# Moving roots, layernorm applications and a residual add between GpSimd, ScalarE and VectorE in a macaron block

## The chip, the cores and the metric

The kernel runs on one core of a Trainium2 chip. A core has five engines that matter here: TensorE (PE in the profile, with its weight loads as PEld), VectorE (DVE), ScalarE (ACT), GpSimd (POOL) and SyncE (SP), which here only issues DMAs. The metric is the device time of one execution in microseconds. The kernel before takes 2504.11 us, the median of three runs (2503.69 to 2505.66).

## The reference: a feed-forward part, attention, a feed-forward part

The input x has 8 batches of 1024 rows of 512 fp32 values. The block computes

```python
x = x + 0.5 * ffn(layernorm(x))
x = x + attention(layernorm(x))
x = x + 0.5 * ffn(layernorm(x))
```

`layernorm` subtracts the mean of a row and divides by the root of its variance plus 1e-5. `ffn` quantises each row and each column of a 512 x 512 matrix to whole numbers between -127 and 127, with the largest absolute value as the scale, multiplies them, and scales the product back by the row's and the column's scale. `attention` projects to q, k and v with 16 heads of 32 values, applies a layernorm with gain and offset to each head of q and k, takes the causal softmax of the scaled products, and projects the result with a bias.

## The kernel before, in words

**Tiles.** A tile is 128 rows of x. `First` (L317) is the first feed-forward part of a tile and the layernorm ahead of attention, `Last` (L353) is attention's output projection and the second feed-forward part, and both inherit the quantised product from `Ffn` (L258). `Norm` (L231) holds a layernorm: `stats` on VectorE, `root` on GpSimd, `apply` on VectorE. `Unit` (L386) is attention for four heads of one batch; there are 32 units. A unit's work has three phases that run in three successive stages: projection of q, k and v with their norms (`project`, `take`, `squares`, `logs`, `divide`, `turn`), row maxima of the scores (the `m_` functions), and exponentials with sums (the `e_` functions).

**Order.** The order on each engine is the program's, written out by hand. Each engine works through its own list in that order. After an opening loop for ten `First` tiles (L680 to L704) comes a plan of stages k = -1 to 32 of 20 steps each (L737 to L836). Stage k runs the `e_` phase of unit k, the `m_` phase of unit k+1 and the projection of unit k+2. `at(k, s, rank, fn)` puts a function at a step; one with a step past 19 falls into the next stage. Inside a step the order is by rank, FILL, SUM, MISC, REST, BULK, ADD, and inside a rank by the order of the calls to `at`.

For the change, this is who stands where:

- FILL: scores of both phases on TensorE, then `m_max` (VectorE), the exponential (ScalarE, L589) and, on diagonal blocks, the causal select (GpSimd, L593).
- SUM: `e_sum` (the product with v, L621) in even steps, and `e_den` (L635) in steps 10 and 22, that is 2 of the next stage. `e_den` writes `p_d` and copies it out on ScalarE (L647).
- MISC: `turn` (L452) in steps 11, 13, 21 and 23; `flip` (L296), `product` (L303) and `spread` (L345) of the feed-forward tiles.
- REST: everything else of the tiles and norms. BULK: projections. ADD: `e_add` (GpSimd, L609) and, in steps 17 and 18, `m_wide`, `m_turn`, `m_shift`.

A stage has two `First` tiles for k = -1 to 25 and two `Last` tiles for k = 4 to 31. Stages 4 to 25 have both.

**Buffers.** PSUM is divided by tags. `ps_e` and `ps_m` hold scores, `ps_p` (two buffers) projections. `ps_x` (L199) is one bank with one buffer. `turn`, `e_den`, and in the stages also `flip`, `product` and `spread` of all tiles but those of the last batch take it in turn: each user's first matmul waits until the engine that reads the user before it has finished.

Of the kernel before, what the change touches and what calls it, by code (L numbers as in the profile page):

```python
# [9 lines left out]
F32 = mybir.dt.float32  # L10
# [5 lines left out]
P = 128  # L16
# [39 lines left out]
def macaron_kernel(  # L56
# [51 lines left out]
    nc.vector.memset(ones_bf, 1.0)  # L108
    eps = const.tile([P, 1], F32, name="eps")
    nc.vector.memset(eps, EPS)  # L110
    mhalf = const.tile([P, 1], F32, name="mhalf")
    nc.vector.memset(mhalf, -0.5)
# [118 lines left out]
    class Norm:  # L231
# [26 lines left out]
    class Ffn:  # L258
# [44 lines left out]
        def product(self):  # L303
# [5 lines left out]
            self.f = self.tile([P, E], F32, "f")  # L309
            nc.vector.scalar_tensor_tensor(self.f, p_f, self.hsc, rs_bc, ALU.mult, ALU.mult)  # L310

        def add(self):
            nc.gpsimd.tensor_tensor(self.f, self.f, self.src, ALU.add)  # L313

# [71 lines left out]
    class Unit:  # L386
# [44 lines left out]


        def logs(self, j):
            lv = small.tile([P, 16], F32, tag="hlv", name=f"hlv_{self.u}_{j}")
            nc.scalar.activation(lv, self.ss, AF.Ln, scale=1.0 / HD, bias=eps)
            self.r0 = small.tile([P, 16], F32, tag="hr0", name=f"hr0_{self.u}_{j}")
            nc.scalar.activation(self.r0, lv, AF.Exp, scale=-0.5)

        def divide(self, j):
            tag = f"{self.u}_{j}"  # L440
            ss, r0, c = self.ss, self.r0, self.cs[j]
            nc.vector.tensor_scalar(ss, ss, 1.0 / HD, EPS, ALU.mult, ALU.add)
            h = small.tile([P, 16], F32, tag="hh", name=f"hh_{tag}")
            nc.vector.scalar_tensor_tensor(h, r0, -0.5, r0, ALU.mult, ALU.mult)
            nc.vector.tensor_tensor(h, h, ss, ALU.mult)
            r = small.tile([P, 16], F32, tag="hr", name=f"hr_{tag}")
            nc.vector.scalar_tensor_tensor(r, h, 1.5, r0, ALU.add, ALU.mult)
            c = c.rearrange("p t s d -> p (t s) d")
            nc.vector.tensor_tensor(c, c, r.unsqueeze(2).to_broadcast([P, 16, HD]), ALU.mult)

# [245 lines left out]
    for j in range(NT // 2):  # L696
        for i, fn in ((15, "squares"), (15, "logs"), (16, "divide"), (17, "turn")):
            extra[2 * j + i].append((getattr(units[0], fn), j))
# [45 lines left out]
    def last(f, k, s0):  # L744
        at(k, s0, BULK, f.project, 0)
        at(k, s0 + 1, BULK, f.project, 1)
        for s, rank, fn in (
            (-1, REST, f.load),
            (2, REST, f.begin),
            (3, REST, f.root),  # L750
            (4, REST, f.scale),
            (5, REST, f.whole),
            (6, MISC, f.flip),
            (7, MISC, f.product),
            (8, REST, f.add),
            (9, REST, f.store),
# [3 lines left out]
    for k in range(-1, NU + 1):  # L760
# [44 lines left out]
        if 0 < b < B and (b, j) != (1, 0):  # L805
            for n in range(2):
                f = First(b, 2 * j + n, ps_x, bufs)
                for s, rank, fn in (
                    (2, REST, f.load),
                    (4, REST, f.begin),  # L810
                    (5, REST, f.root),
                    (6, REST, f.scale),
                    (7, REST, f.whole),
                    (8, MISC, f.flip),
                    (9, MISC, f.product),
                    (10, REST, f.add),
                    (11, REST, f.store),
# [60 lines left out]
```

## Time and profile before

| | us |
|---|---|
| median of three runs | 2504.11 |
| the profiled execution | 2508.39 |
| its span | 2506.7 |
| PE busy | 2392.0 (95%) |
| DVE busy | 1778.8 (71%) |
| POOL busy | 1681.9 (67%) |
| ACT busy | 1237.1 (49%) |

Instructions that the change touches, by line and mean duration:

| Line | What | Count | Mean, ns |
|---|---|---|---|
| L251 | layernorm applied, DVE: tile's input, before attention, second part | 64 each | 640, 978, 599 |
| L310 | product scaled out of PSUM, DVE | 128 | 744 |
| L313 | residual added, POOL | 128 | 1405 and 1420 |
| L435, L437 | logarithm and exponential for the norm's root, ACT, 16 columns | 128 each | 322, 216 |
| L442, L444, L445, L447 | refinement of that root, DVE, 16 columns | 128 each | 216, 194, 259, 483 |
| L248 | a power on POOL, one column | 192 | 572 to 577 |
| L535 | row maxima spread for the transposes, ACT | 32 | 1056 |

Busy times are sums of instruction durations; they can overlap on TensorE, where matmuls are pipelined. A wait is listed with the engine and line that ended it. In the middle of the execution a stage takes 73.6 us and stages repeat to within a few hundredths of a microsecond.

### The profile page before, as it was taken

What the parts mean: (1) busy time and instruction counts of PE and PEld (TensorE: products, weight loads), DVE (VectorE), ACT (ScalarE), POOL (GpSimd) and SP (SyncE); (2) the same over time, 40 slices, a digit from 0 to 9 for tenths busy, and PEclk for the clock granted to TensorE, in tenths of its full rate; (3) what the DMA queues carried; (4) which work ended last, traced back from release to release, by engine and by line L of the source; (5) the groups of instructions that cost most, each with busy time, mean ns of one, the idle gap of its engine ahead of it and who ended that gap; (6) DMA issues with size and microseconds to landing.
All of it is one profiled execution on the core that took longest, in us unless ns stands there. A gap on an engine that the chain in (4) does not pass through costs nothing.

```text
span 2506.7 us, 40820 instructions
## 1 busy us (share of the span) xinstructions
PE 2392.0 (95%) x15448; PEld 1099.6 (44%) x15448; DVE 1778.8 (71%) x3053; ACT 1237.1 (49%) x2409; POOL 1681.9 (67%) x1790
## 2 busy tenths in 40 slices
PE   3999999999999999999999999999999999999785
PEld 1544444444444444444444444444444444444332
DVE  9566777777777777777777777777777776666664
ACT  2335555555554555555555555555555555545441
POOL 3227777776777776677777667777767776666672
PEclk9899999999999999999999999999999999999997
DMA  4000000111110111111011111111111100000011
GB/s 143 30 18 22 27 26 27 31 41 38 33 42 31 43 35 35 39 35 43 31 43 35 35 39 35 43 32 35 44 35 39 35 28 25 27 27 27 26 43 59
DMA packets 79303, 92.86 MB, mean 37 GB/s; under 512 B 30977, under 2 KB 37121, under 8 KB 79106
## 3 DMA queue, kind: packets, MB, share of 16 engines
q1 hardware_dynamic: 79106, 90.26, 11.8%
q8 instruction: 121, 1.98, 0.3%
q14 instruction: 76, 0.62, 0.1%
HBM read 55.60 MB, written 34.08 MB: 36 GB/s over the span
## 4 chain that ended last, share of the span: by engine, by line
PE 76%; DVE 12%; POOL 7%; issue 4%; SPq 1%; ACT 1%; DMA 1%; DVEq 0%; POOLq 0%; ACTq 0%
PE p_qkv L402 22%; PE p_s L496 17%; PE p_o L621 9%; PE p_w_b L370 8%; PE p_t L566 6%; POOL pt L609 4%; DVE nm L523 3%; PE p_f_b L306 2%; PE p_d L639 2%; PE p_s L480 2%; PE p_f_a L306 2%; PE p_h L456 2%; POOL f_b L313 2%; DVE oT L674 1%; PE p_m L543 1%
## 5 line engine op out<-in xcount | busy, mean ns | idle before, releaser
L609 POOL TENSOR_TENSOR pt<-pt,pt 128x768 f32<-128x768 f32 (+1 forms) x630 | 1109.7, 1764 | 127.0 <-ACT pt L589 108.5
L589 ACT ACTIVATE pt<-p_t 128x1024 f32<-128x1024 f32 (+1 forms) x640 | 599.4, 938 | 982.4 <-PE p_t L566 908.4
L523 DVE TENSOR_REDUCE nm<-p_s 128x2 f32<-128x1024 f32 (+2 forms) x640 | 632.9, 1006 | 525.8 <-PE p_t L566 409.6
L402 PE MATMUL p_qkv<-wall,yT_a 128*128 128x384 f32 x2048 | 773.7, 501 | 0.2 <-ACT v L421 0.2
L496 PE MATMUL p_s<-qk 32*128 32x512 f32 (+3 forms) x3072 | 656.6, 524 | 14.1 <-DVE nm L523 12.4
L566 PE MATMUL p_t<-qk 32*128 32x512 f32 (+3 forms) x3072 | 663.2, 526 | 2.0 <-ACT pt L589 2.0
L402 PEld LDWEIGHTS p_qkv<-wall,yT_a 128*128 128x128 f32 x2048 | 354.7, 191 | 287.3 <-issue 136.6
L593 POOL TENSOR_SCALAR_AFFINE_SELECT pt<-pt 128x256 f32<-128x256 f32 x512 | 227.6, 457 | 215.6 <-ACT pt L589 214.2
L621 PE MATMUL p_o<-pt,v 128*32 128x512 f32 (+3 forms) x3072 | 340.7, 497 | 11.8 <-POOL pt L593 11.6
L496 PEld LDWEIGHTS p_s<-qk 32*128 32x128 f32 x3072 | 227.5, 185 | 198.0 <-DVE nm L523 65.6
L566 PEld LDWEIGHTS p_t<-qk 32*128 32x128 f32 x3072 | 238.7, 183 | 52.2 <-ACT pt L589 23.5
L370 PE MATMUL p_w_b<-wo,oT 128*128 128x512 f32 x512 | 244.3, 600 | 0.0
L621 PEld LDWEIGHTS p_o<-pt,v 128*32 128x32 f32 x3072 | 75.1, 108 | 247.8 <-issue 159.0
L313 POOL TENSOR_TENSOR f_a<-f_a,xin_a 128x512 f32<-128x512 f32 x64 | 90.9, 1420 | 84.2 <-DVE f_a L310 84.2
L480 PEld LDWEIGHTS <-ident_bf 128*128 128x128 bf16 x1024 | 83.5, 98 | 135.9 <-issue 81.2
L462 ACT ACTIVATE qk<-p_h,qk_b,qk_g 128x256 f32<-128x256 f32 x256 | 130.1, 563 | 11.9 <-PE p_h L456 11.9
L370 PEld LDWEIGHTS p_w_b<-wo,oT 128*128 128x128 f32 x512 | 97.6, 192 | 78.0 <-issue 69.1
L480 PE MATMUL p_s<-causal_bf,ident_bf 128*128 128x128 bf16 x1024 | 110.2, 220 | 8.6 <-DVE nm L523 5.8
L514 DVE TENSOR_REDUCE nm<-p_s 128x4 f32<-128x1024 f32 x64 | 77.6, 1212 | 47.2 <-PE p_t L566 42.6
L417 ACT ACTIVATE sq<-p_qkv 128x256 f32<-128x256 f32 x256 | 99.1, 387 | 21.7 <-PE p_qkv L402 15.1
L420 ACT COPY c<-p_qkv 128x256 f32<-128x256 f32 x256 | 96.8, 378 | 4.3 <-PE p_h L456 4.3
L313 POOL TENSOR_TENSOR f_b<-f_b,x_b 128x512 f32<-128x512 f32 x64 | 89.9, 1405 | 8.9 <-DVE f_b L310 8.9
(108 smaller groups left out, 2474.0 us busy)
## 6 DMA issues: line engine op xcount, KB each, us to landing
xin_a<-in_x_dram SPq DMA_DIRECT2D x64, 256.0 KB, 2.8
x1d_a<-f_a SPq DMA_DIRECT2D x64, 256.0 KB, 2.2
rb<-rdr SPq DMA_DIRECT2D x256, 64.0 KB, 2.0
x1r_b<-x1d_a SPq DMA_DIRECT2D x64, 256.0 KB, 2.9
out_dram<-f_b SPq DMA_DIRECT2D x64, 256.0 KB, 2.1
dsq<-dsb SPq DMA_DIRECT2D x256, 2.0 KB, 1.7
rT<-in_rhsT_dram SPq DMA_DIRECT2D x4, 256.0 KB, 3.6
wall<-in_wqT_dram SPq DMA_DIRECT2D x4, 256.0 KB, 5.8
```

Source lines behind the costliest of these rows:

```text
L313: nc.gpsimd.tensor_tensor(self.f, self.f, self.src, ALU.add)
L370: nc.tensor.matmul(self.p_w, oT[self.b, g, hf][:, o : o + P], wo[:, g, :], start=False, stop=(g == NG - 1),)
L402: nc.tensor.matmul(self.p[:, : 3 * P], yT[self.b, t][:, kc, :], wall[:, kc, self.g].rearrange("p a f -> p (a f)"), start=(kc == 0), stop=( ...
L462: nc.scalar.activation(self.qk[:, a, 2 * j * P : (2 * j + 2) * P], p_h[:, a].rearrange("p t i -> p (t i)"), AF.Identity, scale=qk_g[:, a : ...
L480: nc.tensor.matmul(self.pm[:, hh, c0 + n - P : c0 + n], ident_bf, causal_bf, start=not self.pm_begun, stop=False, skip_group_check=True,)
L496: nc.tensor.matmul(self.pm[:, hh, c0 : c0 + n], self.rows(0, h, it * P, P), self.rows(1, h, ch * HALF, n), start=not self.pm_begun and sub ...
L523: nc.vector.tensor_reduce(self.nm[:, ch, it, hs], self.pm[:, :, c0 : c0 + n], AX.X, ALU.max, negate=True)
L566: nc.tensor.matmul(self.pes[pr][:, hh, c0 : c0 + n], self.rows(1, h, jt * P, P), self.rows(0, h, hf * HALF + o, n), start=True, stop=True, ...
L589: nc.scalar.activation(pt[:, :, :cols], self.pes[pr][:, :, :cols], AF.Exp, scale=scale)
L593: nc.gpsimd.affine_select(out=pt[:, :, c0 : c0 + P], in_=pt[:, :, c0 : c0 + P], compare_op=ALU.is_ge, fill=0.0, base=0, pattern=[[0, 2], [ ...
L609: eng.tensor_tensor(acc[:, :, o : o + n], acc[:, :, o : o + n], pt[:, :, c0 : c0 + n], ALU.add)
L621: nc.tensor.matmul(self.p_o[h * HD : (h + 1) * HD, o : o + n], self.v[:, jt, h * HD : (h + 1) * HD], self.pt[i, h // 2][:, h % 2, c0 : c0 ...
```

## The change

There are three exchanges between engines and a re-timing that goes with them.

1. `logs` and the refinement in `divide` are replaced by `roots`, which adds the epsilon and takes the power -0.5 of 16 columns on GpSimd. `divide` keeps only its last multiplication.
2. `Norm.apply` becomes one ScalarE instruction with scale rstd and a per-row offset; `root` computes this offset on GpSimd. In the feed-forward part `apply` moves out of `scale` into a step of its own, `norm`, and all that follows, up to `product`, comes one step later.
3. `add` on GpSimd goes. `product` multiplies the PSUM tile in place by the column scales and then, in a second VectorE instruction, by the row scale with the residual added. `store` keeps its step.
4. `m_wide` moves from step 17 (last rank) to step 18 (MISC).

```diff
         def root(self):
-            nc.gpsimd.tensor_tensor(self.rstd, ve, mhalf, ALU.pow)
+            nc.gpsimd.tensor_tensor(self.rstd, ve, mhalf[:, 0:1], ALU.pow)
+            self.off = small.tile([P, 1], F32, tag="off", name=f"off_{self.tag}", bufs=8)
+            nc.gpsimd.tensor_scalar(
+                self.off, self.mv[:, 0:1], self.rstd, -1.0, ALU.mult, ALU.mult
+            )
         def apply(self, dst):
-            nc.vector.tensor_scalar(
-                dst, self.src, self.mv[:, 0:1], self.rstd, ALU.subtract, ALU.mult
-            )
+            nc.scalar.activation(dst, self.src, AF.Identity, scale=self.rstd, bias=self.off)
...
+        def norm(self):
+            self.y = self.tile([P, E], F32, "y")
+            self.ln.apply(self.y)
         def scale(self):
-            self.y = self.tile([P, E], F32, "y")
-            self.ln.apply(self.y)
...
-            nc.vector.scalar_tensor_tensor(self.f, p_f, self.hsc, rs_bc, ALU.mult, ALU.mult)
-        def add(self):
-            nc.gpsimd.tensor_tensor(self.f, self.f, self.src, ALU.add)
+            nc.vector.tensor_tensor(p_f, p_f, rs_bc, ALU.mult)
+            nc.vector.scalar_tensor_tensor(self.f, p_f, self.hsc, self.src, ALU.mult, ALU.add)
...
-        def logs(self, j):
-            lv = small.tile([P, 16], F32, tag="hlv", name=f"hlv_{self.u}_{j}")
-            nc.scalar.activation(lv, self.ss, AF.Ln, scale=1.0 / HD, bias=eps)
-            self.r0 = small.tile([P, 16], F32, tag="hr0", name=f"hr0_{self.u}_{j}")
-            nc.scalar.activation(self.r0, lv, AF.Exp, scale=-0.5)
+        def roots(self, j):
+            ve = small.tile([P, 16], F32, tag="hve", name=f"hve_{self.u}_{j}")
+            nc.gpsimd.tensor_scalar(ve, self.ss, 1.0 / HD, EPS, ALU.mult, ALU.add)
+            self.r = small.tile([P, 16], F32, tag="hr", name=f"hr_{self.u}_{j}")
+            nc.gpsimd.tensor_tensor(self.r, ve, mhalf, ALU.pow)
         def divide(self, j):
-            nc.vector.tensor_scalar(ss, ss, 1.0 / HD, EPS, ALU.mult, ALU.add)
-            nc.vector.scalar_tensor_tensor(h, r0, -0.5, r0, ALU.mult, ALU.mult)
-            nc.vector.tensor_tensor(h, h, ss, ALU.mult)
-            nc.vector.scalar_tensor_tensor(r, h, 1.5, r0, ALU.add, ALU.mult)
             nc.vector.tensor_tensor(c, c, r.unsqueeze(2).to_broadcast([P, 16, HD]), ALU.mult)
...
-    parts = "load begin root scale whole flip product add store root2 norm2 spread".split()
+    parts = "load begin root norm scale whole flip product store root2 norm2 spread".split()
...
     def last(f, k, s0):
-            (4, REST, f.scale), (5, REST, f.whole),
-            (6, MISC, f.flip), (7, MISC, f.product), (8, REST, f.add),
+            (4, REST, f.norm), (5, REST, f.scale), (6, REST, f.whole),
+            (7, MISC, f.flip), (8, MISC, f.product),
             (9, REST, f.store),
...
-            at(k, 17, ADD, mu.m_wide)
+            at(k, 18, MISC, mu.m_wide)
...
-                at(k, s + 2, REST, pu.logs, j)
+                at(k, s + 2, REST, pu.roots, j)
...
     (First, in the stages)
-                    (6, REST, f.scale), (7, REST, f.whole),
-                    (8, MISC, f.flip), (9, MISC, f.product), (10, REST, f.add),
+                    (6, REST, f.norm), (7, REST, f.scale), (8, REST, f.whole),
+                    (9, MISC, f.flip), (10, MISC, f.product),
                     (11, REST, f.store), (12, REST, f.root2), (13, REST, f.norm2),
                     (16, MISC, f.spread),
```

More of the change, by code (lines that the diff above doesn't have):

```diff
@@ L108, in macaron_kernel @@
     nc.vector.memset(ones_bf, 1.0)
-    eps = const.tile([P, 1], F32, name="eps")
-    nc.vector.memset(eps, EPS)
-    mhalf = const.tile([P, 1], F32, name="mhalf")
+    mhalf = const.tile([P, 16], F32, name="mhalf")
     nc.vector.memset(mhalf, -0.5)
@@ L430, in squares @@
             )
[L433 to L449 removed]
+        def roots(self, j):
[3 more added lines that the diff above has]
+            nc.gpsimd.tensor_tensor(self.r, ve, mhalf, ALU.pow)
+        def divide(self, j):
+            c = self.cs[j].rearrange("p t s d -> p (t s) d")
+            nc.vector.tensor_tensor(
+                c, c, self.r.unsqueeze(2).to_broadcast([P, 16, HD]), ALU.mult
+            )
         def turn(self, j):
@@ L696, in macaron_kernel @@
     for j in range(NT // 2):
-        for i, fn in ((15, "squares"), (15, "logs"), (16, "divide"), (17, "turn")):
+        for i, fn in ((15, "squares"), (15, "roots"), (16, "divide"), (17, "turn")):
             extra[2 * j + i].append((getattr(units[0], fn), j))
@@ L750, in last @@
             (3, REST, f.root),
[L751 to L755, printed above, removed]
+            (4, REST, f.norm),
+            (5, REST, f.scale),
+            (6, REST, f.whole),
+            (7, MISC, f.flip),
+            (8, MISC, f.product),
             (9, REST, f.store),
@@ L811, in macaron_kernel @@
                     (5, REST, f.root),
[L812 to L816, printed above, removed]
+                    (6, REST, f.norm),
+                    (7, REST, f.scale),
+                    (8, REST, f.whole),
+                    (9, MISC, f.flip),
+                    (10, MISC, f.product),
                     (11, REST, f.store),
```

## The prediction, made before the changed kernel had run

> **What bounds the kernel now.** I read the row of busy tenths on the page first, then busy times by stretch of time, then the timelines of single engines inside one stage, because the row alone can't say whether a busy TensorE is merely waiting inside its pipeline. The columns of the second fence are the stretch, its length, and busy time (with counts) of PE, PEld, DVE, ACT and POOL.
>
> ```profile
> PE   3999999999999999999999999999999999999785
> ```
>
> ```profile
> 218.50:284.50 66.00, 64.40 (x450) 29.48 (x448) 47.48 (x76) 36.16 (x73) 47.58 (x49) 1.00 0.09 26
> 1444.50:1518.00 73.50, 72.90 (x483) 33.76 (x482) 54.19 (x94) 38.36 (x75) 53.07 (x57) 1.00 0.12 37
> 2180.00:2253.00 73.00, 73.00 (x482) 33.72 (x484) 45.90 (x74) 35.56 (x70) 49.05 (x49) 1.00 0.08 23
> ```
>
> TensorE is busy for all but 0.6 us of a 73.5 us stage; VectorE has 19 us free, GpSimd 20, ScalarE 35. In the PE timeline of one stage (start, duration, instruction) each group starts where the one before stops feeding, some 0.07 us ahead of its listed end:
>
> ```profile
> 1418.67 1.06 PE L621 MATMUL p_o<-pt,v 128*32 128x512 f32 x8
> 1419.56 1.04 PE L639 MATMUL p_d<-pt,ones 128*32 128x512 f32 x8
> 1420.53 1.56 PE L402 MATMUL p_qkv<-wall,yT_a 128*128 128x384 f32 x4
> ...
> 1431.87 0.70 PE L496 MATMUL p_s<-qk 32*128 32x512 f32 x2 [0.19 <-DVE nm L523]
> ...
> 1440.13 1.06 PE L621 MATMUL p_o<-pt,v 128*32 128x512 f32 x8
> 1441.13 0.66 PE L348 MATMUL p_y_a<-ident,y_a 128*128 128x128 f32 x4
> 1441.62 1.46 PE L402 MATMUL p_qkv<-wall,yT_a 128*128 128x384 f32 x4
> ```
>
> Measured that way, PE loses only 0.79 us in the stage from 1370 to 1444: 0.13 and 0.26 waiting for a row maximum (the second is the marked line), and 0.40 waiting for GpSimd's causal select, in step 18. POOL's timeline shows why: the residual add and a sum stand ahead of that select.
>
> ```profile
> 1369.65 1.55 POOL L313 TENSOR_TENSOR f_b<-f_b,x_b 128x512 f32<-128x512 f32 x1
> 1371.16 2.35 POOL L609 TENSOR_TENSOR pt<-pt,pt 128x1024 f32<-128x1024 f32 x1
> 1373.47 0.78 POOL L593 TENSOR_SCALAR_AFFINE_SELECT pt<-pt 128x256 f32<-128x256 f32 x2
> ```
>
> So in the middle, busy time taken from VectorE can return at most 0.79 us a stage. A new PE wait, however, adds its full length. The two ScalarE lines that decide are these:
>
> ```profile
> 1420.66 0.59 ACT L647 COPY dsb<-p_d 128x512 f32<-128x512 f32 x1 [0.74 <-PE p_d L639]
> ...
> 1441.82 0.59 ACT L350 COPY yT_a<-p_y_a 128x512 f32<-128x512 f32 x1 [0.42 <-PE p_y_a L348]
> ```
>
> They empty `ps_x`, while PE is already on p_qkv, which has another bank.
>
> **What the Trainium skill says.** PSUM — Partial Sum Buffer, section Engine vs sequencer instructions: matmuls start and complete in program order, and the other engines' queues are strict FIFO. The timelines agree: the 0.40 us wait above has everything of PE behind it. The same page, section PSUM bank collisions raise a hardware error, asks that a bank be guarded as a whole, so a second tile in the one `ps_x` bank can't begin under the first one's copy. ScalarE: Activation LUTs, section What ACT_TABLE_LOAD costs, prices an activation at 186 ns plus 0.833 ns an element and about 93 ns for each pointer operand. The trace agrees: 378 ns for a plain copy of 256 columns (L420), 563 with two pointers (L462), so 92 each. GPSIMD Engine Reference, section 3.1, makes GpSimd's cost per element grow with the operations that an element takes; it prices no power.
>
> **The change part by part, in a stage with both kinds of tile.**
>
> *Work moved.* VectorE loses 2 x 0.64 + 2 x 0.98 + 2 x 0.60 = 4.4 us (L251) and 4 x (0.22 + 0.19 + 0.26 + 0.48) = 4.6 us (L442 to L447), and gains four in-place multiplications. None is shown with PSUM as output; the nearest row (L380, PSUM and SBUF in) is 0.68 us, so 2.7 us. Its second instruction is L310's kind, 0.74 us as before. Net -6.3 us. ScalarE loses 4 x 0.54 and gains six applications at 634 (L294, 512 columns from SBUF) + 2 x 92 = 0.82 us: net +2.8, to 41 of 73.5 us. GpSimd loses four adds of 1.41 = 5.6, gains six offsets at 0.24 (as L246) = 1.4, and four times R, the cost of `roots`. All this lies beside PE, except through GpSimd's select and the waits below. If that cover went, VectorE would have to gain 19 us to be the bound. DMAs keep their place on SP's queue; stores only change their producer.
>
> *ps_x, the deciding step.* Its users by step before: 1 turn, 2 den, 3 turn, 4 flip (Last), 5 product (Last), 6 spread, 8 flip (First), 9 product (First), 10 den, 11 and 13 turn, 14 and 15 flip and product (Last), 16 spread, 18 and 19 flip and product (First). Never are there two in a step, and a score fill and mostly a projection stand between. Flip and product move one step on, but den, spread and turn don't. So `product` now falls on den in step 10 and on spread in steps 6 and 16. In step 10 SUM goes before MISC; in 6 and 16 both are MISC and `First` is entered before `Last`. In each case product follows the other directly on PE, and waits for its ScalarE copy. What PE would lose is read from the lines above: 1420.66 + 0.59 - 1420.53 = 0.72 us after den, 1441.82 + 0.59 - 1441.62 = 0.79 after spread. To restart adds 0.05 (the marked L496 starts at 1431.87, the maximum before it ended at 1431.82), and up to 0.10 for product's weight load (L306) if this waits too. I take the middle, 0.82 and 0.89. Den meets product in stages 0 to 25, 26 times; spread meets it 22 times in step 16 (stages 4 to 25) and 22 times in step 6, a stage later. 26 x 0.82 + 44 x 0.89 = **+60.5 us** (57 to 64). Queued behind are the projection and all later scores. VectorE meets the late product in step 10 ahead of `x_b` and its statistics; they start some 2 us later in their step, which takes what the missing refinement gives, so I leave the two waits for maxima as they are. Turn in step 11 comes 2.5 us after product ends, the two VectorE instructions need 1.4: no wait.
>
> *Stages -1 to 3, First alone.* Steps 8 and 9 have no projection there. PE lost 0.19 us after step 8's flip and 0.64 after step 9's product, waiting for `m_max`. Flip now leaves step 8 and product step 9, replaced by flip: the waits grow by 0.33 and 0.64, since the maximum sets the pace. Steps 18 and 19 lose similarly some 0.4 us. Five stages by 1.4: **+7**.
>
> *GpSimd in step 18.* R is unknown. One column of power takes 574 ns; the sums (L609: 840, 1342, 1812, 2412 ns for 256 to 1024 columns) point to some 0.3 us for a one-column add, so one column of power costs up to 0.3 us more. If that is a start-up cost R is about 0.27 + 0.57 = 0.84 us; if paid for each of 16 columns, 0.27 + 0.27 + 16 x 0.3 = 5.3 us. I take the geometric middle, 2 us. Roots in step 16 stand in POOL's continuous stretch that ends in the late select. The select's lateness was 0.40; +0.3 for an offset, +R, -1.5 for the add that is gone, +0.4 for `hsc` one step later, -0.89 for the wait that PE already had in step 16: R - 1.3 = 0.7 us. That is +0.3 x 22 = **+7**. Stages 0 to 3 have no second-part add to lose: +1.5 x 4 = **+6**.
>
> *m_wide.* It ended at 1374.64, held by the minimum from VectorE; in step 18 it can run after the exponential by the same time, and `m_turn` came at 1377.09: 0, with 2 us of cover from the p_w projection. Without it (stages 0 to 3) it is in the 0.4 above.
>
> *Ends.* From 15 to 65 us VectorE is the bound (47.2 of 50 us busy): -8.9 (14 applications) + 4.8 (7 multiplications), of which some stays hidden: -3. Stage 30 and the last 100 us lose 13 and 28 us on PE to VectorE, GpSimd and latency in turn: four adds of 1.2 on the chain go, four multiplications of 0.7 come, and an application is 0.2 us longer: -5. Together **-8** (0 to -15).
>
> Sum: 60.5 + 7 + 7 + 6 - 8 = +72 us, on the profiled 2508.4 (span 2506.7 and 1.7 around it) 2580; that execution is 4.3 above the median, so the forecast for the runs is 2504 + 72 = **2576**. With R = 0.84 it is +50 (2554), with 5.3 some +160 (2664).
>
> **Rivals.**
> *A: the power is paid per column* (R near 5.3). GpSimd then has 53.1 - 5.6 + 1.4 + 21 = 70 of 76 us, in-order waits included too much: the select comes 4 us late in every stage, 2664. For: the 0.3 us excess on one column. Against: nothing in the trace has more than one.
> *B: faster; GpSimd and VectorE relief outweighs.* Place: steps 12 to 18 and both ends. It would have to return all 0.79 x 26 = 21 us, the ends' 8 to 15 and some of stage 30's 13: at most 45 us. It decides if a collision costs under 0.5 us instead of 0.85, with R under 1. Then about 2490. Against: both copies' ends are fixed to 0.01 us over the stages.
> *C: the waits don't come*, product being placed where PE has other work first: then +12 - 21, about 2500, no change or slightly faster. Against: the ranks.
>
> **How the numbers follow.** Likeliest case, R between 0.8 and 3: 0.66, 2545 to 2600. A: 0.25, 2600 to 2690. B: 0.06. C: 0.03, of which 0.02 within 0.2%. A measurement of this kernel can tell about 0.2%, 5 us, from no change. Below 2538 lie B, C and a little of the likeliest, above 2662 half of A's upper part: range 2538 to 2662. Faster 0.07, within 0.2% 0.02, slower 0.91.
>
> **What would show it.** Right: PE waiting in L306's place for ScalarE's dsb and yT copies, three times a stage, with 0.8 to 0.9 us each; stages of about 76.4 us in the middle, stages 26 to 29 near 73.0 as before; VectorE some 6 us less busy a stage. Wrong: L306 starting right after p_d or p_y; a power on 16 columns above 3 us (A); PE losing under 1 us in a stage (B or C); or a longer wait on ScalarE for offsets, which I put at nothing because six applications fit in its 35 free microseconds.

## The result, and the profile after

The changed kernel takes 2654.9 us (median of four runs, 2648.1 to 2658.5), the kernel before in the same comparison 2503.9 (2499.0 to 2505.7). The ratio is 1.060, interval 1.058 to 1.062: **slower by 151 us**. The forecast was 2576, range 2538 to 2662. The sign and the range held; the loss is twice the 72 us forecast.

The profiled execution has a span of 2654.7 us. Busy time is 2417.2 for PE (91% of the span, 95% before), 1660.6 for DVE, 1316.0 for ACT and 1964.0 for POOL (1681.9 before). In the page's chain of work PE fell from 76% to 50% of the span, and POOL rose from 7% to 28%. The rows of busy tenths of the kernel after:

```profile
PE   3889888999999999999999999999999999999775
...
POOL 2347787777887877788787778878777887877651
```

A slice is 66.4 us. The stages 0 to 3 lie in slices 3 to 7 of PE, all 9 before; four of the five are 8 now. The windows that answer to the first two of before (columns as there):

```profile
218.50:284.50 66.00, 59.47 (x392) 28.10 (x391) 35.99 (x50) 30.43 (x57) 52.63 (x53) 0.90 0.06 17
1476.00:1553.00 77.00, 73.66 (x478) 33.77 (x482) 50.29 (x75) 40.54 (x74) 61.52 (x66) 1.00 0.12 35
```

In the middle PE, nearly without a gap before, lacks 3.3 of 77 us. In the early window it lacks 6.5 of 66 us and its granted clock is 0.90, where it was 1.00.

The length of every stage, taken from one `m_turn` transpose on PE to the next, shows where the time came from. Each row is the sum over its stages, and the last ends with the last compute instruction, 3.0 us before the end of the span; the forecast is regrouped from the terms of the prediction.

| Stretch | Before, us | After, us | Measured | Forecast |
|---|---|---|---|---|
| up to the first `m_turn` | 160.5 | 163.0 | +2.5 | -1.6 |
| four stages, First alone (0 to 3) | 261.1 | 293.9 | +32.9 | +14.9 |
| 22 stages with both kinds | 1617.6 | 1704.6 | +87.0 | +63.8 |
| five late stages | 344.7 | 359.3 | +14.6 | 0 |
| after the last `m_turn` | 119.7 | 130.8 | +11.1 | -5 |
| sum | 2503.6 | 2651.6 | +148.1 | +72.1 |

**The middle.** In PE's timeline of the kernel after (start, duration, instruction, and in brackets the wait ahead of it):

```profile
1243.13 0.40 PE L473 MATMUL p_s<-causal_bf,ident_bf 128*128 128x128 bf16 x4 [0.56 <-DVE nm L516]
...
1304.23 0.84 PE L614 MATMUL p_o<-pt,v 128*32 128x384 f32 x4
1306.21 1.06 PE L614 MATMUL p_o<-pt,v 128*32 128x384 f32 x12 [1.14 <-POOL pt L586]
...
1492.30 0.66 PE L348 MATMUL p_y_a<-ident,y_a 128*128 128x128 f32 x4
1493.63 1.02 PE L308 MATMUL p_f_b<-rq,qT_b 128*128 128x512 bf16 x3 [0.67 <-ACT yT_a L350]
...
1508.11 1.04 PE L632 MATMUL p_d<-pt,ones 128*32 128x512 f32 x8
1509.85 1.02 PE L308 MATMUL p_f_a<-rq,qT_a 128*128 128x512 bf16 x3 [0.70 <-ACT dsb L640]
```

The two meetings on `ps_x` are there, in the last two pairs of lines: `product` directly after spread and after den, waiting for the ScalarE copy. The list of waits of the kernel after counts them (us in total, times, longest):

```profile
PE p_f_b L308 <- ACT yT_a L350: 29.6, 44, 0.7
...
PE p_f_a L308 <- ACT dsb L640: 18.3, 26, 0.7
```

44 and 26 are the numbers of the prediction. From the start of spread to the next start PE takes 1.33 us (1492.30 to 1493.63), where it took 0.49 before (1441.13 to 1441.62 in the prediction's lines); from the start of den 1.74 instead of 0.97. So PE loses 0.84 after spread and 0.77 after den, 44 x 0.84 + 26 x 0.77 = 57 us. The expectations below reckon with 0.73 after spread, and so with 52 us.

The pair at 1304.23 is step 18 of stage 14. The group of 16 matmuls takes 2.97 us, from 1304.23 to 1306.21 + 1.06 with 0.07 of overlap taken off, where it takes 1.01 without a wait: PE loses 1.96 us. It is 2.92 to 2.98 in 17 of the 22 stages and 2.6 in the other five. POOL's and VectorE's timelines of the kernel after say why:

```profile
1300.00 2.93 POOL L436 TENSOR_TENSOR hr<-hve,mhalf 128x16 f32<-128x16 f32 x1
1302.90 2.35 POOL L602 TENSOR_TENSOR pt<-pt,pt 128x1024 f32<-128x1024 f32 x1
1305.21 1.31 POOL L586 TENSOR_SCALAR_AFFINE_SELECT pt<-pt 128x256 f32<-128x256 f32 x2
```

```profile
1305.21 0.68 DVE L440 TENSOR_TENSOR c<-c,hr 128x512 f32<-128x512 f32 x1
```

The roots cost 2.93 + 0.21 = R = 3.14 us, and the select that PE needs stands behind them and a sum. It also begins together with `divide` (L440) and takes 1.31 us, where it took 0.78 before. Before, the same group of matmuls took 2.19, so PE lost 1.18 there.

A third loss, 0.6 us, is a new wait for a row maximum between steps 1 and 2, the first line of PE above. VectorE's timeline of the kernel after shows what stands ahead of this maximum:

```profile
1238.21 0.70 DVE L312 TENSOR_TENSOR p_f_a<-p_f_a,rs_bc 128x512 f32<-128x512 f32 x1 [0.25 <-PE p_f_a L308]
1239.01 0.75 DVE L313 SCALAR_TENSOR_TENSOR f_a<-p_f_a,hsc_a,xin_a 128x512 f32<-128x512 f32 x1
...
1241.82 1.25 DVE L516 TENSOR_REDUCE nm<-p_s 128x2 f32<-128x256 f32 x2
```

The late product, now two instructions, is in front of `oT`, `x_b`, its statistics and then the maximum. Before, it stood ahead of an earlier maximum. So of the 4.05 us that stage 14 is longer, meetings are 2.45, the select 0.78, the maximum 0.6; 0.2 is spread over small differences. Over the 22 stages that is about 54 us for the meetings, 15 for the select and 13 for the maximum.

**The stages 0 to 3.** VectorE's timeline of the kernel after, in one of them:

```profile
266.17 1.22 DVE L516 TENSOR_REDUCE nm<-p_s 128x2 f32<-128x1024 f32 x1 [2.29 <-PE p_t L559]
267.31 1.66 DVE L440 TENSOR_TENSOR c<-c,hr 128x512 f32<-128x512 f32 x1
268.89 0.67 DVE L283 TENSOR_REDUCE amax_a<-y_a 128x1 f32<-128x512 f32 x1
...
269.99 0.49 DVE L290 TENSOR_SCALAR y_a<-y_a,inv_a 128x512 f32<-128x512 f32 x1
270.39 1.28 DVE L516 TENSOR_REDUCE nm<-p_s 128x2 f32<-128x256 f32 x2
```

The last is the row maximum that PE wants. Two things are queued ahead of it. `divide` (L440) took 1.66 us beside a GpSimd sum that began at 267.15, right behind the roots (`divide` takes 0.68 in step 18 above). And `scale` (L283 to L290), which the change moves one step later, now comes in the same step. With the power on one column (e6 below) PE's pause here is 0.84 us instead of 1.82, so about 1.0 of it goes with the power's length. PE's timeline and its clock by stretches of 2 us:

```profile
268.84 1.06 PE L614 MATMUL p_o<-pt,v 128*32 128x512 f32 x8
271.72 0.40 PE L473 MATMUL p_s<-causal_bf,ident_bf 128*128 128x128 bf16 x4 [1.82 <-DVE nm L516]
...
272.06 0.97 PE L559 MATMUL p_t<-qk 32*128 32x512 f32 x2
...
309.84 1.90 PE L614 MATMUL p_o<-pt,v 128*32 128x384 f32 x12 [2.90 <-POOL pt L586]
```

```profile
270.00:272.00 2.00, 0.28 (x4) 0.23 (x4) 1.67 (x3) 1.22 (x4) 2.00 (x2) 1.00 0.00 0
272.00:274.00 2.00, 2.00 (x17) 0.86 (x15) 0.01 (x1) 0.07 (x1) 0.67 (x1) 0.59 0.00 0
274.00:276.00 2.00, 1.00 (x8) 0.70 (x10) 1.87 (x3) 1.43 (x2) 0.04 (x1) 0.50 0.00 0
276.00:278.00 2.00, 2.00 (x12) 0.20 (x8) 0.46 (x1) 0.34 (x1) 1.92 (x2) 0.50 0.00 0
```

This pause of 1.8 us is followed by some 6 us at half clock: two p_t matmuls, 0.70 us at full clock, take 0.97, and others later 1.2. Each of these stages has such a pause and, in step 18, one of 2.9 us for the select (the last line of PE), where at most 0.7 was listed before. By the trace's record of the clock, half clock followed all four pauses of 2.9 us, but only two of the four of 1.8. Over the stages 0 to 3 PE's listed waits are 11.6 us for the select instead of 2.0, 11.7 for maxima instead of 2.8, and 2.8 for den. Matmuls that ran at half clock lost half of their time to it: 13.8 us over these stages (none before), and 10.5 against 6.2 us after the last `m_turn`.

### The profile page after: what moved, and what is told of

Read it like the earlier page. It is cut to its first block, busy times and chain, and to the rows that moved or that the text cites. A ratio compares the mean times of both kernels' runs of the same rounds, so it can differ in the third digit from the quotient of the medians.

```text
span 2654.7 us, 40371 instructions
## 1 busy us (share of the span) xinstructions
PE 2417.2 (91%) x15332; PEld 1107.7 (42%) x15448; DVE 1660.6 (63%) x2476; ACT 1316.0 (50%) x2345; POOL 1964.0 (74%) x2110
## 4 chain that ended last, share of the span: by engine, by line
PE 50%; POOL 28%; DVE 16%; issue 3%; ACT 2%; SPq 1%; DMA 0%; DVEq 0%; ACTq 0%; POOLq 0%
POOL pt L602 15%; PE p_qkv L402 11%; PE p_s L489 10%; PE p_w_b L370 7%; PE p_o L614 6%; POOL hr L436 6%; PE p_t L559 4%; DVE nm L516 4%; DVE y_b L290 3%; POOL pt L586 2%; PE p_s L473 2%; PE p_d L632 2%; PE p_f_b L308 1%; PE p_f_a L308 1%; DVE st_fb L238 1%
## 5 line engine op out<-in xcount | busy, mean ns | idle before, releaser
L602 POOL TENSOR_TENSOR pt<-pt,pt 128x768 f32<-128x768 f32 (+1 forms) x630 | 1089.9, 1731 | 51.5 <-ACT pt L582 41.5
L614 PE MATMUL p_o<-pt,v 128*32 128x512 f32 (+3 forms) x3072 | 347.4, 503 | 40.9 <-POOL pt L586 40.7
L436 POOL TENSOR_TENSOR hr<-hve,mhalf 128x16 f32<-128x16 f32 x128 | 374.9, 2929 | 10.7
L312 DVE TENSOR_TENSOR p_f_b<-p_f_b,rs_bc 128x512 f32<-128x512 f32 x64 | 44.8, 699 | 134.6 <-PE p_f_b L308 132.4
L440 DVE TENSOR_TENSOR c<-c,hr 128x512 f32<-128x512 f32 x128 | 108.6, 848 | 16.2 <-POOL hr L436 16.2
L434 POOL TENSOR_SCALAR hve<-hss 128x16 f32<-128x16 f32 x128 | 27.3, 213 | 111.0 <-DVE hss L428 103.3
```

The costliest lines, as they stand in the source:

```text
L436: nc.gpsimd.tensor_tensor(self.r, ve, mhalf, ALU.pow)
L602: eng.tensor_tensor(acc[:, :, o : o + n], acc[:, :, o : o + n], pt[:, :, c0 : c0 + n], ALU.add)
L614: nc.tensor.matmul(self.p_o[h * HD : (h + 1) * HD, o : o + n], self.v[:, jt, h * HD : (h + 1) * HD], self.pt[i, h // 2][:, h % 2, c0 : c0 ...
```

## The experiments

Where an expectation names theories by letters, P stands for the power on GpSimd and S for the later steps with their meetings. All times are medians; ratios are to the kernel before in the same comparison.

### Putting one part back

**e1: the kernel after with the logarithms and the refinement back.**

```diff
-                at(k, s + 2, REST, pu.roots, j)
+                at(k, s + 2, REST, pu.logs, j)
```
(`logs`, the longer `divide` and `eps` are those of the kernel before.)

> Theory P (the power on GpSimd, 3.14 us for each call of roots with its epsilon, costs most of what the three meetings on ps_x don't): without it the changed kernel falls by about 90 us, to 2560 to 2575, and the 2.9 us waits of p_o in stages 0 to 3 and the 1.9 us waits for row maxima there go. Theory S (the later steps of flip and product cost the rest, the power little): it falls by 25 us or less, to 2630 or more.

Measured 2695.5 us (2691.3 to 2697.3), ratio 1.075 (1.073 to 1.078): 40 us slower than after, so neither theory holds as it stood. A part of VectorE's and PE's timelines of e1, one fence each:

```profile
1294.51 2.29 DVE L446 TENSOR_TENSOR hh<-hh,hss 128x16 f32<-128x16 f32 x1
```

```profile
1299.71 1.22 PE L497 MATMUL p_s<-qk 32*128 32x512 f32 x2 [2.32 <-DVE nm L524]
```

An instruction on 16 columns, 0.17 us elsewhere, took 2.29 beside a GpSimd sum of 2.35 us that had begun 0.1 us earlier. The maximum behind it came late, PE paused 2.3 us, and two score matmuls then took 1.22 instead of 0.70. That is a mechanism that neither theory had: an instruction on VectorE can be held up by one on GpSimd.

**e2: the kernel after with the second part's `product` behind the projection.** Both meetings are taken away.

```diff
-            (8, MISC, f.product),
+            (8, ADD if k < NU - 2 else MISC, f.product),
...
-                at(k, s, SUM, eu.e_den, hf)
+                at(k, s, ADD if s == 10 else SUM, eu.e_den, hf)
```

> The product of a Last tile stands behind the step's projection and den of step 10 behind its projection, so that product no longer directly follows den or spread. If the meetings cost what the trace of the changed kernel shows (26 x 0.77 + 44 x 0.73 = 52 us on PE), it falls to 2600 to 2610. If another wait takes their place (rows maxima, the select), it falls by 20 us or less.

Measured 2681.0 us (2680.0 to 2683.7), ratio 1.070 (1.068 to 1.072): slower than after by 26. The waits of L308 for `yT` and `dsb` are gone (48 us in the list of waits), but PE's waits for row maxima grew from 44 to 87 us and for the select from 41 to 57. So a wait on PE doesn't simply add its length, as the prediction took it to. Two readings remain, and this run doesn't separate them: PE came earlier to waits that the meetings had covered, or the moved product and den came later for VectorE.

**e6: the kernel after with the power on one column only**, the other 15 roots a constant, so that the output isn't the reference's.

```diff
-            nc.gpsimd.tensor_tensor(self.r, ve, mhalf, ALU.pow)
+            nc.gpsimd.tensor_scalar(self.r, self.ss, 0.0, 0.12, ALU.mult, ALU.add)
+            nc.gpsimd.tensor_tensor(self.r[:, 0:1], ve[:, 0:1], mhalf[:, 0:1], ALU.pow)
```

> The changed kernel with the power taken of one column only; the other 15 roots are a constant, so the output isn't the reference's. A call of roots then takes about 1.05 us on GpSimd in place of 3.14. If the length of the power is what the early stages, the select in step 18 and the stages from 26 on suffer from: 45 to 65 us less than the changed kernel's 2655, that is 2590 to 2610, no wait of p_o above 1 us, and the granted clock at 1.00 in stages 0 to 3. If the later steps make these waits: 2635 or more.

Measured 2609.9 us (2608.8 to 2612.8), ratio 1.042 (1.040 to 1.044): 45 us of the 151 go with 15 columns of power, as expected. The power on one column takes 559 ns here, on 16 it takes 2929. The four stages 0 to 3 give 14 us of it, most of that their clock (matmuls lost 3.3 us to it instead of 13.8), the 22 of the middle 25. Waits for the select of 2.2 us remained in the early stages, and half clock after two of the four, which was not expected.

### Doing one part alone

**e5: the kernel before with the residual on VectorE**, nothing else; `add` is gone and all steps are the old ones.

```diff
-            nc.vector.scalar_tensor_tensor(self.f, p_f, self.hsc, rs_bc, ALU.mult, ALU.mult)
-        def add(self):
-            nc.gpsimd.tensor_tensor(self.f, self.f, self.src, ALU.add)
+            nc.vector.tensor_tensor(p_f, p_f, rs_bc, ALU.mult)
+            nc.vector.scalar_tensor_tensor(self.f, p_f, self.hsc, self.src, ALU.mult, ALU.add)
```

> The kernel before with the residual added by VectorE alone, product in its old step. By the prediction's parts the 0.40 us wait for the select in step 18 goes and the ends gain a little: 10 to 15 us faster, about 2490. Rival: the extra 0.70 us on VectorE in the product's step delays row maxima and takes it back: within 5 us of 2504.

Measured 2481.0 us (2479.2 to 2482.5), ratio 0.990 (0.988 to 0.992): **faster than both kernels**, by 26 us than before and 174 than after. Step 18 in PE's timeline of the kernel before, and of e5:

```profile
1372.75 0.84 PE L621 MATMUL p_o<-pt,v 128*32 128x384 f32 x4
1373.93 1.06 PE L621 MATMUL p_o<-pt,v 128*32 128x384 f32 x12 [0.34 <-POOL pt L593]
```

```profile
1360.68 1.07 PE L619 MATMUL p_o<-pt,v 128*32 128x384 f32 x16
```

Before, the group of 16 is cut in two: from 1372.75 to 1374.92, where the next instruction feeds, 2.17 us pass. In e5 it runs in one piece of 1.01. That is 1.16 us, and the stage is 72.41 instead of 73.57. Without the add the select is in time; VectorE's busy time rises from 54.3 to 55.7 us a stage, and that stays beside PE.

**e4: the kernel before with the roots on GpSimd**, add and steps as they were.

```diff
-                at(k, s + 2, REST, pu.logs, j)
+                at(k, s + 2, REST, pu.roots, j)
```

> The kernel before with the roots alone on GpSimd, all steps as they were. Theory P: 80 to 100 us slower than before, 2585 to 2605, since GpSimd still has the residual adds. Theory S: up to 30 us slower.

Measured 2713.6 us (2713.2 to 2718.5), ratio 1.083 (1.081 to 1.085): +206. Roots, add and a sum now stand in one row ahead of the select. PE's timeline and the windows of e4:

```profile
1321.15 1.92 PE L615 MATMUL p_o<-pt,v 128*32 128x384 f32 x12 [3.53 <-POOL pt L587]
...
1323.84 3.35 PE L370 MATMUL p_w_b<-wo,oT 128*128 128x512 f32 x4
```

```profile
1320.00:1324.00 4.00, 2.85 (x18) 1.48 (x19) 0.00 (x0) 0.35 (x1) 3.92 (x6) 0.50 0.21 72
1324.00:1328.00 4.00, 4.00 (x15) 1.89 (x13) 0.00 (x0) 0.96 (x4) 2.89 (x4) 0.65 0.00 0
```

A wait of 3.5 us that ends at 1321.15, and around its end 8 us with a clock of 0.50 to 0.65 (the p_w_b group takes 3.35 instead of 1.88). PE ran for 2.85 of the first 4 us and for all of the next, so the clock took 2.85 x 0.50 + 4 x 0.35 = 2.8 us more. In every second stage the slow stretch is half as long, 3.4 us.

**e7: the kernel before with scale, whole, flip and product one step later**; the add stays where it was, so it now waits for a product of the same step.

```diff
-            (4, REST, f.scale), (5, REST, f.whole), (6, MISC, f.flip), (7, MISC, f.product),
+            (5, REST, f.scale), (6, REST, f.whole), (7, MISC, f.flip), (8, MISC, f.product),
...
-                    (6, REST, f.scale), (7, REST, f.whole), (8, MISC, f.flip), (9, MISC, f.product),
+                    (7, REST, f.scale), (8, REST, f.whole), (9, MISC, f.flip), (10, MISC, f.product),
```

> The kernel before with scale, whole, flip and product one step later and nothing else. By the meetings on ps_x alone: 26 x 0.77 + 44 x 0.73 = 52 us, and about 1 us a stage for the stages of First alone, so 2555 to 2570. If later steps also bring other waits (row maxima behind a late product on VectorE): 2580 or more. If something else of the change makes the meetings dear: 2530 or less.

Measured 2675.0 us (2672.7 to 2677.3), ratio 1.067 (1.066 to 1.069): +168. It can't be read as the price of the steps alone: GpSimd waits 252 us for `f_a`, 84 before. So the steps were tried again on e5, which has no add (e10).

**e8: e5 with `norm2`, one of the three layernorm applications, on ScalarE.**

```diff
-            self.ln2.apply(self.ay)
+            self.ln2.apply_act(self.ay)
```
(`apply_act` is the change's `apply`; `root` computes the offset for this norm alone.)

> The kernel with the residual on VectorE, old steps, and the layernorm ahead of attention (norm2) alone applied on ScalarE. It takes 0.98 us off VectorE between two row maxima in step 13: the waits of 0.23 and 0.25 us for maxima around there shrink, 2465 to 2475. Rival: the extra GpSimd and ScalarE work delays selects and exponentials instead, 2480 to 2500.

Measured 2497.4 us (2492.2 to 2502.0), ratio 0.997 (0.996 to 0.998): 16 us slower than e5. Taking 0.98 us from VectorE, twice a stage, and giving GpSimd an offset instead is a loss here. In the profiled execution, 20 us longer than that of e5, 8.4 us are in the four stages 0 to 3.

**e9: the kernel after with old roots and old steps**: residual on VectorE and all applications on ScalarE, with `root` in the step of the statistics.

```diff
-            (3, REST, f.root), (4, REST, f.norm), (5, REST, f.scale), (6, REST, f.whole),
-            (7, MISC, f.flip), (8, MISC, f.product),
+            (2, REST, f.root), (3, REST, f.norm), (4, REST, f.scale), (5, REST, f.whole),
+            (6, MISC, f.flip), (7, MISC, f.product),
```
(The first part likewise; `m_wide` back in step 17; roots as in e1.)

> All of the change but the roots and the later steps: residual on VectorE, applications on ScalarE one step ahead of scale (the root moves up into the step of the statistics), flip, product and m_wide where they were. If the later steps made the changed kernel without its roots slow (2695): 2470 to 2500. If handing VectorE's work through GpSimd and ScalarE is itself the cost, since all three queues are in order: 2550 or more.

Measured 2592.6 us (2590.7 to 2594.2), ratio 1.034 (1.033 to 1.036): 112 us slower than e5, 103 faster than e1. The stages 0 to 3 are as before (260 us). In the middle PE waits 2.6 us for a maximum in steps 12 and 13, and its matmuls lose 33 us to the clock; VectorE's 16-column instructions (L443, L446) take 0.6 us on average instead of 0.2, its quantising of y_b (L292) 1.4 instead of 0.5. The applications have no free ride either, though e9 also moves the root by a step, which wasn't tried apart.

### The later steps by themselves

**e10: e5 with the later steps and `m_wide` in step 18**: residual on VectorE, old roots, old applications.

```diff
-            (6, MISC, f.flip), (7, MISC, f.product),
+            (7, MISC, f.flip), (8, MISC, f.product),
...
-            at(k, 17, ADD, mu.m_wide)
+            at(k, 18, MISC, mu.m_wide)
```
(`scale`, `whole` and the first part's steps as in e7.)

> The kernel with the residual on VectorE (2481) plus the later steps of scale, whole, flip and product and m_wide in step 18, old roots and old applications. If the later steps cost their meetings on ps_x alone: 2481 + 52 = 2533, up to 2545. If they also put VectorE's work beside GpSimd's sums and row maxima, as the run with the later steps alone suggests (where an add that waited on product also stood in GpSimd's queue): 2590 to 2640.

Measured 2719.9 us (2719.2 to 2720.6), ratio 1.085 (1.083 to 1.087): +239 on e5, far above both expectations. Every stage of the middle is about 81 us instead of 72.4. VectorE's, POOL's and PE's timelines of e10, one fence each:

```profile
1307.44 0.70 DVE L310 TENSOR_TENSOR p_f_a<-p_f_a,rs_bc 128x512 f32<-128x512 f32 x1 [2.43 <-PE p_f_a L306]
...
1310.35 0.18 DVE L242 BATCH_NORM_AGGREGATE mv_fb<-st_fb 128x2 f32<-128x6 f32 x1
...
1311.56 2.81 DVE L672 TENSOR_TENSOR oT<-oU,rb 128x512 f32<-128x512 f32 x1
...
1316.41 1.19 DVE L521 TENSOR_REDUCE nm<-p_s 128x2 f32<-128x1024 f32 x1
```

```profile
1310.92 0.57 POOL L248 TENSOR_TENSOR rstd_fb<-ve_fb,mhalf 128x1 f32<-128x1 f32 x1
1311.46 2.36 POOL L607 TENSOR_TENSOR pt<-pt,pt 128x1024 f32<-128x1024 f32 x1
```

```profile
1317.66 0.70 PE L494 MATMUL p_s<-qk 32*128 32x512 f32 x2 [2.34 <-DVE nm L521]
...
1319.40 2.77 PE L400 MATMUL p_qkv<-wall,yT_a 128*128 128x384 f32 x4
```

The chain reads from the top. The product met den and came late; VectorE stood 2.43 us ahead of it with everything else queued behind. The statistics of `x_b` ended late, at 1310.53; they released GpSimd's root, and the sum queued behind that root began at 1311.46, just ahead of VectorE's `oT`. `oT` then took 2.81 us, as long as the sum and 0.5 more. In e5 the sum had begun at 1192.01 and `oT` comes near its end; VectorE's timeline of e5:

```profile
1193.87 1.04 DVE L672 TENSOR_TENSOR oT<-oU,rb 128x512 f32<-128x512 f32 x1
```

The maximum in step 12 was late by this sum, PE paused 2.34 us, and the projection after it ran at half clock (2.77 instead of 1.46). The Trainium skill, page SBUF — State Buffer, section Who interferes with whom, states that VectorE instructions with two SBUF inputs, or in a mode that takes both ports, and GpSimd instructions that read SBUF exclude each other for a whole instruction, and that issue order decides who blocks. That agrees with 2.81 for `oT` and 2.29 in e1: both have two SBUF inputs, and both began 0.1 us after the sum. PE's pause of 2.34 us is in each of the 22 middle stages, half clock behind it in 17 of them.

**e12: e10 with product and den apart**, by the two lines of e2.

```diff
+            (8, ADD if k < NU - 2 else MISC, f.product),
...
+                at(k, s, ADD if s == 10 else SUM, eu.e_den, hf)
```

> Residual on VectorE and later steps, but product of Last tiles and den of step 10 behind the step's projection, so that no product meets den or spread. If the meetings are a cost of their own: 40 to 55 us below the run with them. If the later product then makes other waits, as in the changed kernel: equal to it or slower.

Measured 2635.0 us (2632.9 to 2640.7), ratio 1.052 (1.050 to 1.053): 85 us faster than e10, more than the meetings' 57. VectorE's wait for the product falls from 2.43 to 0.81 us, and the middle's loss to the clock from 29 us to none. So here a meeting costs more than its wait on PE. Still 154 us on e5 remain. The middle's stages are 77.2 us, with no single large wait: 1.3 in step 0 for the select, 0.6 in step 2, 0.55 in step 6, 1.0 in step 12 for maxima. `oT` still takes 2.00 us beside a sum, at 1270.29.

**e13: e10 with `oT` of the second half one step later**, out of the sum's way.

```diff
-            at(k, (15 if k == NU - 1 else 20, 31)[hf], REST, eu.e_mult, hf)
+            at(k, (15 if k == NU - 1 else 20, 32)[hf], REST, eu.e_mult, hf)
```

> The run with the residual on VectorE and the later steps (2720), with the second half's oT multiplication (two inputs in SBUF) moved from step 11 to step 12, so that it no longer meets GpSimd's sum that the late statistics release. If that meeting (2.81 us in place of 0.7 to 1.0) makes PE's 2.3 us wait for the row maximum in step 12 and the low clock behind it: the wait shrinks to about 0.3 us and the run falls by 50 to 75 us. If VectorE is merely late from its wait for product, and the order of its work doesn't matter: it falls by 15 us or less.

Measured 2710.4 us (2707.5 to 2714.1), ratio 1.081 (1.079 to 1.084): 9.5 us faster than e10, which by the expectation would clear `oT`. The trace says otherwise. VectorE's timeline and POOL's of e13:

```profile
1305.84 2.30 DVE L440 TENSOR_SCALAR hss<-hss 128x16 f32<-128x16 f32 x1
...
1311.21 2.81 DVE L672 TENSOR_TENSOR oT<-oU,rb 128x512 f32<-128x512 f32 x1
```

```profile
1305.74 2.36 POOL L607 TENSOR_TENSOR pt<-pt,pt 128x1024 f32<-128x1024 f32 x1
...
1311.12 2.35 POOL L607 TENSOR_TENSOR pt<-pt,pt 128x1024 f32<-128x1024 f32 x1
```

Another instruction in VectorE's queue was caught in `oT`'s place, and `oT` itself met the next sum. PE's pause shrank only from 2.3 to 1.7 us. The middle lost 3 us to the clock instead of 29, but other waits took most of that back. A reading that fits, not tried by itself: it matters little which instruction stands there, as long as GpSimd's sum is released by VectorE's statistics and so starts among what follows them. The 2.30 us are a `tensor_scalar` with one input; the trace doesn't show in which mode it ran.

**e11: e10 with the roots on GpSimd**, so the kernel after without the applications on ScalarE.

```diff
-                at(k, s + 2, REST, pu.logs, j)
+                at(k, s + 2, REST, pu.roots, j)
```

> The same with the roots on GpSimd: the changed kernel without its applications on ScalarE. If the roots cost here what the short power saved or more: 45 to 80 us above the run without them. If taking the refinement off VectorE pays for the power, as it did between the changed kernel and the one with its roots back: within 10 us of it, or below.

Measured 2744.9 us (2741.2 to 2749.3), ratio 1.095 (1.093 to 1.097): +25 on e10. The kernel after is 90 us below it, so at these steps the applications on ScalarE are worth 90 us with the new roots, and 24 with the old (e10 to e1). At the old steps they cost 112 (e5 to e9, with the root a step earlier). A reading, argued from the timelines and not tried by itself: in the kernel after, `off` stands between the root and the sum. POOL's and VectorE's timelines of the kernel after:

```profile
1515.16 1.26 POOL L248 TENSOR_SCALAR off_fb<-mv_fb,rstd_fb 128x1 f32<-128x1 f32 x1
1516.38 2.36 POOL L602 TENSOR_TENSOR pt<-pt,pt 128x1024 f32<-128x1024 f32 x1
```

```profile
1515.09 0.68 DVE L667 TENSOR_TENSOR oT<-oU,rb 128x512 f32<-128x512 f32 x1
1515.69 0.68 DVE L440 TENSOR_TENSOR c<-c,hr 128x512 f32<-128x512 f32 x1
```

Here `oT` began first. It was GpSimd's short instruction that was held up, to 1.26 us instead of 0.26, and the long sum began only when `oT` and `c` were through. VectorE lost nothing.

All together, with the residual on VectorE in each:

| Roots | Applications | Old steps, us | Later steps, us |
|---|---|---|---|
| old | VectorE | 2481 (e5) | 2720 (e10) |
| GpSimd | VectorE | not tried | 2745 (e11) |
| old | ScalarE | 2593 (e9) | 2695 (e1) |
| GpSimd | ScalarE | not tried | 2655 (after) |

The later steps cost 239 us or 103, the roots +25 or -40, the applications +112, -24 or -90. The later steps include `m_wide` in step 18 here, which wasn't tried alone. The parts don't add up, and no one of them is "the" cause. Shown is that the residual's move gains by itself, and that roots, applications and later steps each lose when laid on it or on the kernel before. By which waits is shown for the meetings, the select and the power's length; for the rest the waits are named, not separated.

## Why the prediction was half right

*Direction and the meetings.* Right. The meetings came in the steps named, 44 and 26 times, at 0.84 and 0.77 us instead of 0.89 and 0.82: 57 us instead of 60.5. That is the copy's end and the restart of 0.05 alone (0.79 + 0.05 and 0.72 + 0.05), without anything for product's weight load. The prediction has the PSUM page ask for a bank guarded as a whole; its rule is by bank and quadrant, and by bank as the simple version, which is the same here, since the tiles in `ps_x` span all 128 partitions. A forecast applied layernorm took 0.82 us (817 to 840 ns measured), an in-place multiplication 0.68 (0.70). ScalarE's busy time rose by 2.4 us a stage in the middle (2.8 forecast), but VectorE's fell by only 3.9 (6.3 forecast). Rival B's mechanism, relief that outweighs, is real for one part: e5 has it. In the whole change it was buried.

*Where the other 76 us are.* By the table above, 23 in the middle, 18 in the stages 0 to 3, 15 in the late stages and 20 at the two ends. The meetings are not among them. What failed is the step from "all this lies beside PE" to nothing else being lost: the prediction's sum has no term for new waits on maxima in the middle, none for the late stages and none for the clock, and too small a one for the power. That the result lies within the range is in part luck. The upper part of the range was there for a select up to 4 us late; the select costs only 0.7 us a stage more in the middle, and other losses fill the gap.

*"VectorE meets the late product in step 10 ... so I leave the two waits for maxima as they are."* This step failed. It priced the late product as 2 us of shift on an engine with 19 us free. In the changed kernel the late product makes a new wait for a maximum, in steps 1 to 2 rather than near step 10: 0.6 us in each stage of the middle, 13 us. What can also shift is which GpSimd sum starts against which VectorE instruction. With the later steps alone on e5 the loss was 239 us, of which the forecast meetings are 57 (e10); with the meetings apart 154 remain (e12). The changed kernel loses less; that its offsets and roots take the sum out of the way is the reading given at e11, not shown. Free time on an engine said nothing on how long its next instruction takes.

*R.* The middle value of 2 us was chosen; it is 3.14. Rival A was right in kind: from one column to 16 the power takes (2929 - 574) / 15 = 157 ns more for each column. The estimate of up to 0.3 us for a column was an upper bound and was used only as one. On the select in step 18 the forecast was 0.7 - 0.4 = 0.3 us more, with R = 3.14 it would be 1.8 - 0.4 = 1.4, and measured is 0.7 on average. With R = 3.14 the prediction's own sum would be 72 + 26 x 1.14 = 102 us: a right R alone would have left 49 of the 151. All in all the power's length costs 45 us (e6), much of it in places where the prediction didn't look for it.

*"PE loses only 0.79 us in the stage", 0.40 of it in step 18.* Misread. The 0.40 was taken as the select's lateness; inside the group of 16 matmuls PE lost 1.18 us. So the residual's move, which entered as 1.5 us off the select's lateness, had 1.16 us a stage to give, and e5's 26 us are those.

*Stages with First alone, +7 and +6.* Measured +32.9 for four stages against 14.9 with den's part. The forecast had the waits for `m_max` grow by 0.33 and 0.64, since flip and product leave steps 8 and 9, but counted neither that `scale` comes into the same step as `divide`, nor that a GpSimd sum holds `divide` up (PE waits 1.82 instead of 0.13 there). The select's 2.9 us exceed its +1.5, and the clock, 13.8 us, was not in it at all.

*Late stages 0, ends -8.* Measured +14.6 and, with the start, +13.6. The roots still run in the late stages: the select in step 18 costs 0.8 there and a maximum in step 12 another 0.9. The prediction gives these stages 73.0 us, which is the length of its window; before, they took 69.5 to 70.7, and 71.9 to 75.1 now. In the last stretch 4.3 of the 11.1 us are matmuls at a lower clock; the rest is not settled.

*The clock* was counted nowhere. The Trainium skill, page TensorE: Matmul & The Clock Gate, section HAM oscillation — how this bites in real kernels, puts the limit for idle gaps at about 3.4 us. The runs here show half clock after listed pauses of 1.8 to 2.3 us already. In the 14 profiled executions of this case, from 145 to 2330 us, it came during or within 3.4 us of none of 1108 gaps of PE between 0.3 and 1.0 us, of 4 of 136 between 1.0 and 1.5, 25 of 113 up to 2.0, 46 of 102 up to 2.5, 27 of 37 up to 3.0, and all 23 longer ones. The measurement decides: in this kernel a pause of about 2 us may cost more than its length, and one of 3 us does.

Still open: the exact share of each interaction in the 151 us, where e12's 154 us begin, what `m_wide` does by itself, and how the residual's version would run with only the roots or only the two other applications moved.

## What to carry to other kernels

Where one engine is bound and the others have slack, price a moved instruction by what is next to it in its new queue and what runs beside it on the other engine, not by busy time: who releases a long GpSimd instruction, and which VectorE instruction will be under way then. Try each part of a bundle alone before adding it up: here one part of four gained 1.0% and the bundle lost 6.0%. Before a stage is re-timed, list every user of a single buffer by step and rank, and count a pause of 2 us or more on TensorE at more than its length: in e4 one of 3.5 us cost up to 2.8 us of slow clock on top.

## What the runs showed of the hardware

- A power on GpSimd took 2929 ns for 128 x 16 and 574 ns for 128 x 1.
- A VectorE instruction of 16 columns, 0.16 us by itself, took 2.3 us beside a GpSimd sum that had begun 0.1 us before it. With VectorE first it is GpSimd that waits (1.26 us for an instruction of 0.26).
- Half clock on TensorE followed about a fifth of the pauses of 1.5 to 2.0 us, half of those of 2.0 to 2.5 and all above 3.0. In the middle of the 14 executions each such stretch lasted 3.4 or 6.8 us.
- A VectorE multiplication with PSUM in and out and one SBUF input, 128 x 512, took 699 ns on average.
